# A gated graph layer on one core: the new gate and the convolution's end products summed in PSUM

## The chip, the core and the metric

The kernel runs on one core of a Trainium2 chip. The metric is the device time of one execution in microseconds (us). A core has a matrix engine (TensorE, in the profile PE, with its weight loads as PEld), a vector engine (VectorE, DVE), a scalar engine for activation functions (ScalarE, ACT), GpSimd (POOL) and a queue engine (SyncE, SP). Matrix products land in PSUM[...]; everything else lies in SBUF or in device memory. An engine runs its instructions in their order, and waits on semaphores for the others.

## The reference

There are B = 32 graphs of N = 512 nodes with D = 256 features, all fp32. Each x is normalised and clipped (h = max(layernorm(x), 0)), and a layer of three parts is added to x:

- a convolution along the nodes: a product with a 256 x 256 matrix, batch norm, relu, a convolution with 17 taps over 256 channels, batch norm, plus h, relu: x_conv;
- a message product: A = exp(-distance of three projected features) times the given mask, x_nmp = A times relu(h w_msg + b);
- a gated unit whose input is x_in = (x_conv, x_nmp) and whose state is h:

```python
r = sigmoid(gi_r + gh_r)
z = sigmoid(gi_z + gh_z)
nn_ = tanh(gi_n + r * gh_n)
return (1.0 - z) * nn_ + z * x
```

Here gi are products of x_in (512 inputs) and gh products of h (256 inputs). Only the n gate needs its two parts apart, since r multiplies the second.

## The kernel before

Features lie on partitions and nodes along the free axis. One fp32 matmul of 512 columns shows as two rows in the profile.

**An order written by a planner.** While the program is built, five generators ("rows", "begins", "graphs", "conv", "gates") are advanced one piece at a time, and what a piece emits stands in that order on each engine. The planner keeps its own account of time: `now` for TensorE, `dve.free` and `act.free` for VectorE and ScalarE. A generator yields a time from which it can go on, or a condition. Of those able to go on the planner takes the one that is furthest behind its pace. `later(t, f)` puts a small piece off until the account reaches t, and `fill` adds VectorE's background work (operands, sums) while its queue reaches less than 1.5 us ahead. On the chip nothing but this order and the semaphores is left.

**Convolution (`convolution`, L737; `summed`, L595).** The 17 taps are computed by a fast scheme: the rows are cut into seven groups, and each group has 25 products of transformed weights and inputs. In the first group a product is one bank. In the other six a product has three parts. First `psb` (tile ps_b, a bank of its own in pool `bps`) takes the middle term, and ScalarE copies it to `mid` in SBUF (L803). Then the two end products go to the two banks of `ps_c` (L806 to L808). The finished pair is handed to `summed`, where `both` (L619) adds `mid` to both halves with one VectorE instruction into `n` or `z`. Further VectorE additions, listed in SUMS and run as background, build the outputs y.

**Messages (`graph`, L969).** Per graph: eight message matmuls, then factors of the distance, `kernel_exp` (L861) with four matmuls into four banks (ps_b and three banks of pool `gps`) and four exponentials, masking on VectorE, and the gather products.

**Gates (`gates`, L1003).** Per graph and half o of the features: the products of r, of the hidden part of n (ps_h), of z, and of the input part of n (ps_n). Each takes a bank ps_acc of pool `acc`, which has two. ScalarE takes tanh of r and z, and halves and biases ps_h in place. VectorE computes r = (r + 1) ps_h into SBUF (`reset_hidden`, L1101), then adds ps_n to it (`mix`, L1117), ScalarE takes tanh of r (`mix_next`, L1035), and VectorE makes the output (`mix_last`, L1042). In the very last half the n products are cut into 384 and 128 columns, and VectorE prepares a part of the output early (`mix_ahead`, L1065).

PSUM's eight banks are: one in bps, two in acc, three in gps, two in cps (two bufs for the first group, later one buf of two banks).

Of the kernel before, what the change touches and what calls it, by code (L numbers as in the profile page):

```python
# [8 lines left out]
F32 = mybir.dt.float32  # L9
# [4 lines left out]
P = 128  # L14
# [34 lines left out]
def kernel(  # L49
# [46 lines left out]
    dram = ctx.enter_context(tc.tile_pool(name="dram", bufs=1, space=bass.MemoryType.DRAM))  # L96
    bps = ctx.enter_context(tc.tile_pool(name="bps", bufs=1, space=PSUM))
    acc = ctx.enter_context(tc.tile_pool(name="acc", bufs=2, space=PSUM))
    gps = ctx.enter_context(tc.tile_pool(name="gps", bufs=3, space=PSUM))
# [485 lines left out]
    SUMS = []  # L585
    summed_to = 0
    read = 0

    def sum_all(to=1e9):
        nonlocal summed_to  # L590
        while SUMS and summed_to < to:
            summed_to += 1
            SUMS.pop(0)()

    def summed(g):  # L595
# [10 lines left out]
        def add(dst, a, b, op=ALU.add):  # L606
            SUMS.append(lambda: dve.tensor_tensor(dst, a, b, op=op))

        def copy(dst, src, scale):
            SUMS.append(lambda: later(  # L610
                dve.free + 0.1, lambda: act.activation(dst, src, AF.Copy, scale=scale)
            ))

        def more(dst, a, k, b, op=ALU.add):
            SUMS.append(
                lambda: dve.scalar_tensor_tensor(dst, a, k, b, op0=ALU.mult, op1=op)
            )

        def both(dst, got):  # L619

            ps, mid = got
            if mid is None:
                act.activation(dst, ps, AF.Copy)
                return
            dve.tensor_tensor(
                dst.rearrange("p (h n) -> p h n", h=2), ps, mid[:, None, :].to_broadcast([P, 2, nh]),
                op=ALU.add,
            )

        for j1 in ORDER:  # L630
# [32 lines left out]
            else:  # L663
                for f in range(3):
                    add(y[:, :, f], y[:, :, f], z, ALU.subtract if (f, j1) == (1, 2) else ALU.add)
        SUMS.append(lambda: EVAC.extend(
            (dve.free + 0.3, y, g, b, o) for b in batches(g) for o in range(ND)
        ))
        yield
# [33 lines left out]
    X2, X_AT, XD = [], [], {}  # L703
    at_product = 0
    freed, made, made_at, bank_at = -1, 0, 0.0, 0.0

# [30 lines left out]
    def convolution():  # L737

        nonlocal at_product, cps

        def product(ps, *terms):


            for o in range(ND):
                matmul_sum(
                    ps[:, o * nu : (o + 1) * nu],
                    [
                        (w[:, k, i, o * P : (o + 1) * P], t[:, at + i * (nu + 1) : at + i * (nu + 1) + nu])
                        for k, t, at in terms
                        for i in range(ND)  # L750
                    ],
                )

        done, handed = None, 0.0

        def hand():
            nonlocal done, handed
            if done is not None:
                got, done = done, None
                sums.send(got)  # L760
                handed = dve.free + LAG

        for g in range(NG):
# [3 lines left out]
            if g == 1:  # L767
                first_ctx.close()
                cps = ctx.enter_context(tc.tile_pool(name="cps2", bufs=1, space=PSUM))
            for n in range(25):  # L770
                at_product = m = 25 * g + n
# [11 lines left out]
                for k in (m, m + 1):  # L783
                    if 25 <= k < len(X2) and k not in XD:
                        XD[k] = ends(X2[k], sizes(k // 25)[3])
                        X_AT[k] = dve.free + LAG
                yield max(X_AT[m], W_AT[m], bank_at if g > 0 else 0.0)
                if 25 <= m < 50:
                    third_weight(m)
                    yield W_AT[m]  # L790
                w, x2 = WS[m], X2[m]
                if g == 0:
                    ps, mid = cps.tile([P, N], F32, name="ps_c")[:, :nz], None
                    d0, d1, d2 = (x2[:, 0, :], 0), (x2[:, 1, :], 0), (x2[:, 0, :], 1)
                    product(ps[:, :nh], (0, *d0), (1, *d1))
                    hand()
                    yield now
                    product(ps[:, nh:], (0, *d1), (1, *d2))
                else:
                    psb = bps.tile([P, N], F32, name="ps_b")[:, :nh]  # L800
                    product(psb, (2, x2[:, 1, :], 0))
                    mid = cv.tile([P, NH], F32, name="mid", bufs=2)[:, :nh]
                    act.activation(mid, psb, AF.Copy)  # L803
                    hand()
                    yield handed
                    ps = cps.tile([P, 2, N], F32, name="ps_c")[:, :, :nh]  # L806
                    for k in range(2):
                        product(ps[:, k, :], (k, XD[m][:, k, :], 0))  # L808
                    del XD[m]
                WS[m] = X2[m] = None  # L810
                done = ps, mid
                if g > 0:
                    later(now + 0.3, hand)
                at_product = m + 1
                yield now
            hand()

# [43 lines left out]
    def kernel_exp(at):  # L861

        nonlocal now, bank_at
        pss = [bps.tile([P, N], F32, name="ps_b"), bank(), bank(), bank()]
        for c in range(NT):
# [103 lines left out]
    def graph(b):  # L969

        nonlocal told
        yield lambda: begun > b
# [16 lines left out]
        settle_stores()  # L989
        at = front.tile([P, NT, N], F32, name="at", bufs=1)  # L990
        kernel_exp(at)
        yield act.free + 0.3
# [10 lines left out]
    def gates(b):  # L1003
# [11 lines left out]

        def products(ps, o, g, ks, then=None, of=None):

# [3 lines left out]
            for k in ks:  # L1021
                w, at = sources[k]
                for i in range(ND):
                    matmul(
                        ps, w[:, at + i, cols(o, g)], hT[:, i, :] if k == 0 else x_in[2 * k - 2 + i],
                        start=(k == of[0] and i == 0), stop=(k == of[-1] and i == ND - 1),
                    )
                if k == ks[-1] and then is not None:
                    then()
                if k == 2 and o == ND - 1 and g == 2:  # L1030
                    load_sums(b + 1, 0)
                    load_sums(b + 1, 1)
                yield now

        def mix_next(r, z, o, s):  # L1035
            act.activation(
                r[:, s], r[:, s], AF.Tanh,
                bias=vec[:, _COL["b_ih"] + 2 * ND + o : _COL["b_ih"] + 2 * ND + o + 1],
# [46 lines left out]
        for o in range(ND):  # L1085
# [9 lines left out]

            def hidden_half(ps_h):
                act.activation(ps_h, ps_h, AF.Identity, bias=bn[:, o : o + 1], scale=0.5)

            halves = []

            def reset_hidden():  # L1101
                if halves:
                    dve.scalar_tensor_tensor(r, r, 1.0, halves.pop(), op0=ALU.add, op1=ALU.mult)

            def reset_later(ps_h):
                halves.append(ps_h)
                later(act.free + 0.3, reset_hidden)
# [8 lines left out]

            def mix(s=slice(0, N)):  # L1117
                reset_hidden()
                dve.tensor_tensor(r[:, s], ps_n[:, s], r[:, s], op=ALU.add)
                later(dve.free + 0.3, lambda r=r, z=z, o=o: mix_next(r, z, o, s))  # L1120

# [17 lines left out]

            def hidden():  # L1140
                ps = acc.tile([P, N], F32, name="ps_acc")
                yield from products(ps, o, 2, (0,), lambda: hidden_half(ps))
                reset_later(ps)

            if ps_h is not None:
                reset_later(ps_h)
            elif not is_last(o):
                yield from hidden()
            ps_z = acc.tile([P, N], F32, name="ps_acc")
            yield from products(ps_z, o, 1, (0, 1, 2), update)  # L1150
            if is_last(o):
                later(act.free + 0.2, lambda: mix_ahead(z, o))
                yield from hidden()
            if o == 0:
                load_gates(b + 1)
                load_conv(b + 1)
            else:
                residual(b + 1)
            ps_n = acc.tile([P, N], F32, name="ps_acc")
            if b < B - 1 or o < ND - 1:  # L1160
                yield from products(ps_n, o, 2, (1, 2) if o == 0 else (2, 1), mix)
                continue

            for s in (slice(0, N - P), slice(N - P, N)):
                if s.start > 0:
                    ps_n = acc.tile([P, N], F32, name="ps_acc")
                for j in range(2 * ND):
                    matmul(
                        ps_n[:, s], wih[:, j, cols(o, 2)], x_in[j][:, s],
                        start=(j == 0), stop=(j == 2 * ND - 1),  # L1170
                    )
                mix(s)
                yield now
# [5 lines left out]
    def sum_some():  # L1179
        if not SUMS:  # L1180
            return False
# [203 lines left out]
```

## Time and profile before

| | |
|---|---|
| median of 3 runs | 2104.84 us (2104.28 to 2105.43) |
| span of the profiled execution | 2103.8 us |
| mean granted TensorE clock | 0.994 |
| last TensorE row starts | 7.2 us before the end of the span |
| DVE r<-ps_acc,r (add of ps_n), 128x512 | 63 of 690 ns |
| DVE z or n <-ps_c,mid, 128x540 | 100 of 715 ns, and 50 of 128x544 |
| ACT mid<-ps_b, 128x270 | 100 of 396 ns, and 50 of 128x272 |
| TensorE rows into ps_acc, ps_c, ps_b, ps_g of at,msg | 2304, 3200, 1264, 512 |

The page gives for every engine its busy time and the number of its instructions, then the chain of work that ended last, then groups of instructions. A group reads: line, engine, operation, output<-inputs by the program's names, shapes, count, busy us, mean ns, and the idle time ahead of it with what ended it. Most instructions here have the line of a helper (L136 matmul, L141 transpose, L127 the two engines' wrapper), so groups are told apart by their tiles. The view of waits reads: waiting group, releasing group, total us, times, longest. The timeline reads: start, length, engine, line, operation, tiles, count, and in brackets the idle time ahead.

### The profile page before, as it was taken

How to read it: one execution, taken by the hardware profiler on the slowest of the kernel's cores; microseconds unless marked ns; L12 is line 12 of the kernel's file. 1: busy time of each engine (PE TensorE's matmuls, PEld its weight loads, DVE VectorE, ACT ScalarE, POOL GpSimd, SP SyncE). 2: the span in 40 equal slices, each digit the busy share in tenths (PEclk: the TensorE clock that was granted, in tenths of full speed). 3: DMA queues.
4: the chain of work that ended last, by engine and by line, in shares of the span. 5: the costliest groups of instructions: out<-in, count | busy, mean ns of one | idle time of the engine just before them, and what ended most of it. 6: DMA issues, size and time to landing. Idle time of an engine off the chain costs nothing.

```text
span 2103.8 us, 25938 instructions
## 1 busy us (share of the span) xinstructions
PE 2056.0 (98%) x8776; PEld 1260.3 (60%) x8776; DVE 1509.8 (72%) x2662; ACT 730.9 (35%) x1280; POOL 335.2 (16%) x582
## 2 busy tenths in 40 slices
PE   9999899999999999999999999999999999999998
PEld 5887466665666546656566665456665666654443
DVE  6887499886799668878488865588985877763333
ACT  6543532226322254222443222533224432133111
POOL 2000112112111021011111101211111110112111
PEclk9999999999999999999999999999999999999999
DMA  7446687777875767677776777777777655624332
GB/s 279 162 145 203 249 256 202 199 210 209 228 212 162 223 172 201 175 195 195 227 184 172 189 201 181 217 172 210 211 181 193 180 162 157 170 72 109 86 91 40
DMA packets 546436, 383.07 MB, mean 182 GB/s; under 512 B 456576, under 2 KB 473472, under 8 KB 545664
## 3 DMA queue, kind: packets, MB, share of 16 engines
q1 hardware_dynamic: 512992, 282.17, 51.3%
q0 software_dynamic: 28624, 86.01, 13.0%
q10 hardware_dynamic: 4688, 13.24, 1.6%
q8 instruction: 70, 1.15, 0.2%
q14 instruction: 62, 0.51, 0.1%
HBM read 281.95 MB, written 99.35 MB: 181 GB/s over the span
## 4 chain that ended last, share of the span: by engine, by line
PE 92%; DVE 4%; ACT 2%; DMA 1%; issue 1%; SPq 0%; POOL 0%; ACTq 0%; DVEq 0%
PE ps_acc L136 47%; PE ps_g L136 20%; PE ps_c L136 15%; PE ps_b L136 6%; PE ps_g L141 1%; PE ps_b L867 1%; ACT r L127 1%; DVE gg L127 1%; DVE at L127 1%; DVE y L127 0%; DVE z L127 0%; PE ps_acc L146 0%; ACT y L127 0%; DVE x L127 0%; ACT at L127 0%
## 5 line engine op out<-in xcount | busy, mean ns | idle before, releaser
L136 PE MATMUL ps_acc<-hTb,whh 128*128 128x512 f32 x768 | 357.6, 596 | 13.8 <-ACT r L127 13.5
L136 PE MATMUL ps_acc<-xconv,wih 128*128 128x512 f32 (+1 forms) x772 | 361.8, 591 | 0.0
L136 PE MATMUL ps_acc<-xnb,wih 128*128 128x512 f32 (+1 forms) x772 | 358.6, 591 | 0.0
L136 PEld LDWEIGHTS ps_c<-xd,w 128*128 128x128 f32 x2400 | 294.3, 191 | 31.6 <-issue 27.4
L136 PE MATMUL ps_c<-xd,w 128*128 128x135 f32 (+1 forms) x2400 | 303.5, 279 | 1.9 <-DVE n L127 1.6
L1078 POOL DMA_DIRECT2D out_dram<-res x252 | 164.0, 657 | 634.0 <-DVE res L127 559.4
L136 PEld LDWEIGHTS ps_acc<-hTb,whh 128*128 128x128 f32 x768 | 139.7, 190 | 173.7 <-issue 135.6
L136 PEld LDWEIGHTS ps_acc<-xconv,wih 128*128 128x128 f32 x772 | 142.8, 190 | 158.2 <-issue 156.3
L136 PEld LDWEIGHTS ps_acc<-xnb,wih 128*128 128x128 f32 x772 | 142.7, 190 | 157.1 <-issue 154.7
L136 PE MATMUL ps_g<-at,msg 128*128 128x512 f32 x512 | 228.8, 596 | 1.5 <-DVE at L127 1.5
L136 PEld LDWEIGHTS ps_b<-x,w 128*128 128x128 f32 x1200 | 157.1, 190 | 47.8 <-issue 39.7
L127 DVE TENSOR_TENSOR r<-ps_acc,r 128x512 f32<-128x512 f32 (+1 forms) x65 | 44.3, 682 | 192.5 <-PE ps_acc L136 192.5
L136 PE MATMUL ps_b<-x,w 128*128 128x135 f32 (+1 forms) x1200 | 163.6, 279 | 4.3 <-DMA w<-wd 2.2
L136 PEld LDWEIGHTS ps_g<-at,msg 128*128 128x128 f32 x512 | 96.1, 191 | 113.4 <-issue 108.6
L127 ACT ACTIVATE mid<-ps_b 128x270 f32<-128x270 f32 (+1 forms) x150 | 59.5, 396 | 290.8 <-PE ps_b L136 281.3
L127 DVE TENSOR_TENSOR msg<-ps_g,bmsg 128x256 f32<-128x256 f32 x128 | 53.9, 422 | 123.5 <-PE ps_g L136 123.3
L127 DVE SCALAR_TENSOR_TENSOR x<-x,x 128x544 f32<-128x544 f32 (+5 forms) x161 | 137.8, 856 | 2.9
L136 PE MATMUL ps_g<-hT,w 128*128 128x512 f32 (+4 forms) x288 | 119.9, 564 | 10.8 <-DMA hT<-hd 6.8
L127 DVE TENSOR_TENSOR x<-x 128x272 f32<-128x272 f32 (+5 forms) x280 | 127.4, 498 | 0.2
L136 PE MATMUL ps_g<-wmsg,hTg 128*128 128x259 f32 x496 | 123.5, 382 | 0.3 <-DVE aug L127 0.3
L127 DVE TENSOR_TENSOR xd<-x 128x544 f32<-128x544 f32 (+1 forms) x150 | 106.9, 719 | 23.1 <-PE ps_c L136 22.6
L127 ACT ACTIVATE z<-ps_acc,brz 128x512 f32<-128x512 f32 x64 | 44.0, 687 | 219.1 <-PE ps_acc L136 211.9
(124 smaller groups left out, 2563.4 us busy)
## 6 DMA issues: line engine op xcount, KB each, us to landing
w<-wd SPq DMA_DIRECT2D x125, 768.0 KB, 5.2
m_sb<-in_adj_dram SPq DMA_DIRECT2D x384, 64.0 KB, 3.3
hd<-hT POOLq DMA_DIRECT2D x32, 512.0 KB, 6.1
hT<-hd SPq DMA_DIRECT2D x32, 512.0 KB, 4.8
hTb<-hd SPq DMA_DIRECT2D x32, 512.0 KB, 5.4
xnb<-nd SPq DMA_DIRECT2D x64, 256.0 KB, 3.5
xconv<-cd SPq DMA_DIRECT2D x32, 512.0 KB, 5.6
res<-in_x_dram SPq DMA_DIRECT2D x256, 64.0 KB, 3.3
```

What stands on the lines that cost most here:

```text
L127: getattr(self.engine, name)(*tiles, **more)
L136: nc.tensor.matmul(ps, lhsT, rhs, **more)
L141: nc.tensor.transpose(ps, a, ident)
L867: nc.tensor.matmul(pss[c], gr.left[k, :], gr.right[k, :], start=True, stop=True, tile_position=(32 * c, 0),)
L1078: queue.dma_start(OB[b][:, s.start // 32 : s.stop // 32, o * P + 32 * g : o * P + 32 * g + 32], y[at, s].rearrange("i (k j) -> i k j", j=32),)
```

## The change

Values that VectorE or ScalarE wrote into a bank stay there, and further matmuls add onto them (start=False).

- Gates: VectorE writes (r + 1) ps_h back into ps_h's bank, and the input products of n are added onto it; ScalarE takes tanh straight from the bank. ps_n and VectorE's addition are gone. Ahead of the n products the generator yields until VectorE's planned time. `acc` has three banks.
- Convolution: the middle term goes into the first bank of ps_c, ScalarE copies it into the second, and the end products are added onto both. ps_b and `mid` are gone; `both` is now one ScalarE copy of the pair, and the next product waits for it. One seed matmul at the start of the second group writes the second bank once.
- `kernel_exp` takes its fourth bank from `acc` in the first group and from `ps_c` later, with two flags that keep it and a product apart.
- Sums in SUMS carry the time from which they may run.
- The very last half computes ps_h in two parts (384 and 128 columns), with n's products added after both.

```diff
-    bps = ctx.enter_context(tc.tile_pool(name="bps", bufs=1, space=PSUM))
-    acc = ctx.enter_context(tc.tile_pool(name="acc", bufs=2, space=PSUM))
+    acc = ctx.enter_context(tc.tile_pool(name="acc", bufs=3, space=PSUM))
...
-        def both(dst, got):
-
-            ps, mid = got
-            if mid is None:
-                act.activation(dst, ps, AF.Copy)
-                return
-            dve.tensor_tensor(
-                dst.rearrange("p (h n) -> p h n", h=2), ps, mid[:, None, :].to_broadcast([P, 2, nh]),
-                op=ALU.add,
-            )
+        def both(dst, ps):
+
+            nonlocal bank_at, sums_at
+            act.activation(dst.rearrange("p (h n) -> p h n", h=2), ps, AF.Copy)
+            bank_at = sums_at = act.free + LAG
...
+                ps = cps.tile([P, 2, N], F32, name="ps_c")
+                matmul(ps[:, 1, :NH], ident, h1[:, :NH], start=True, stop=True)
+                wide = True
...
-                    psb = bps.tile([P, N], F32, name="ps_b")[:, :nh]
-                    product(psb, (2, x2[:, 1, :], 0))
-                    mid = cv.tile([P, NH], F32, name="mid", bufs=2)[:, :nh]
-                    act.activation(mid, psb, AF.Copy)
-                    hand()
-                    yield handed
+                    in_product = True
                     ps = cps.tile([P, 2, N], F32, name="ps_c")[:, :, :nh]
+                    product(ps[:, 0, :], (2, x2[:, 1, :], 0), clear=(True, False))
+                    act.activation(ps[:, 1, :], ps[:, 0, :], AF.Copy)
+                    yield act.free + LAG
                     for k in range(2):
-                        product(ps[:, k, :], (k, XD[m][:, k, :], 0))
+                        product(ps[:, k, :], (k, XD[m][:, k, :], 0), clear=(False, False))
...
                 yield now
+                if g > 0:
+                    yield lambda: done is None
...
-        pss = [bps.tile([P, N], F32, name="ps_b"), bank(), bank(), bank()]
+        exp_waits = False
+        if not wide:
+            extra = acc.tile([P, N], F32, name="ps_acc")
+        else:
+            extra = cps.tile([P, 2, N], F32, name="ps_c")[:, 0, :]
+        pss = [extra, bank(), bank(), bank()]
...
+        if in_product:
+            exp_waits = True
+            yield lambda: not in_product
+            yield bank_at
         kernel_exp(at)
...
             def reset_hidden():
-                if halves:
-                    dve.scalar_tensor_tensor(r, r, 1.0, halves.pop(), op0=ALU.add, op1=ALU.mult)
+                while halves:
+                    ps, s = halves.pop(0)
+                    dve.scalar_tensor_tensor(
+                        ps[:, s], r[:, s], 1.0, ps[:, s], op0=ALU.add, op1=ALU.mult
+                    )
...
-            def mix(s=slice(0, N)):
-                reset_hidden()
-                dve.tensor_tensor(r[:, s], ps_n[:, s], r[:, s], op=ALU.add)
-                later(dve.free + 0.3, lambda r=r, z=z, o=o: mix_next(r, z, o, s))
+            def mix(ps_n, s=slice(0, N)):
+                later(now + 0.3, lambda r=r, z=z, o=o: mix_next(r, ps_n, z, o, s))
...
-            ps_n = acc.tile([P, N], F32, name="ps_acc")
-            if b < B - 1 or o < ND - 1:
-                yield from products(ps_n, o, 2, (1, 2) if o == 0 else (2, 1), mix)
+            if not is_last(o):
+                reset_hidden()
+                yield dve.free + 0.1
+                yield from products(
+                    ps_h, o, 2, (1, 2) if o == 0 else (2, 1), lambda: mix(ps_h), clear=False
+                )
                 continue
 
+            later(act.free + 0.2, lambda: mix_ahead(z, o))
+            parts = []
             for s in (slice(0, N - P), slice(N - P, N)):
-                if s.start > 0:
-                    ps_n = acc.tile([P, N], F32, name="ps_acc")
+                ps = acc.tile([P, N], F32, name="ps_acc")
+                parts.append((ps, s))
+                for i in range(ND):
+                    matmul(
+                        ps[:, s], whh[:, i, cols(o, 2)], hT[:, i, s],
+                        start=(i == 0), stop=(i == ND - 1), skip_group_check=True,
+                    )
+                hidden_half(ps, s)
+                reset_later(ps, s)
+                yield now
+            settle()
+            yield dve.free + 0.1
+            for ps, s in parts:
                 for j in range(2 * ND):
                     matmul(
-                        ps_n[:, s], wih[:, j, cols(o, 2)], x_in[j][:, s],
-                        start=(j == 0), stop=(j == 2 * ND - 1),
+                        ps[:, s], wih[:, j, cols(o, 2)], x_in[j][:, s],
+                        start=False, stop=(j == 2 * ND - 1), skip_group_check=True,
                     )
-                mix(s)
+                mix(ps, s)
                 yield now
...
     def sum_some():
-        if not SUMS:
+        if not SUMS or SUMS[0][0] > max(now, dve.free) + 0.1:
             return False
```

## The prediction

> **What bounds the kernel now.** I read the page's busy table first, then who TensorE waited for, then the timeline around the waits.
>
> ```profile
> span 2103.8 us, 25938 instructions
> PE 2056.0 (98%) x8776; PEld 1260.3 (60%) x8776; DVE 1509.8 (72%) x2662; ACT 730.9 (35%) x1280; POOL 335.2 (16%) x582
> PE 92%; DVE 4%; ACT 2%; DMA 1%; issue 1%; SPq 0%; POOL 0%; ACTq 0%; DVEq 0%
> ```
>
> TensorE sets the end: 98% busy and 92% of the chain. VectorE (72%) and ScalarE (35%) matter only where TensorE waits for them. The change leaves TensorE's work as it is, so it can win or lose only TensorE's stalls. How much is there? The busy figure hides short stalls, because a matmul's modelled end lies past its slot. The starts tell more:
>
> ```profile
> 2067.88 1.88 PE L136 MATMUL ps_acc<-xconv,wih 128*128 128x512 f32 x4
> 2069.60 1.88 PE L136 MATMUL ps_acc<-xnb,wih 128*128 128x512 f32 x4
> 2072.26 1.98 PE L136 MATMUL ps_acc<-hTb,whh 128*128 128x512 f32 x4 [0.78 <-ACT r L127]
> 2074.08 1.88 PE L136 MATMUL ps_acc<-xconv,wih 128*128 128x512 f32 x4
> ```
>
> Four 512-column rows take 1.72 us from start to start (0.43 each, while one row shows 0.59). After 2069.60 the next should start at 2071.32; it starts at 2072.26 and its own four take 1.82. So a shown idle of 0.78 costs 1.04: idle, plus 0.16 of modelled end, plus 0.10 of slower restart. I add 0.27 to each idle from here on. In the same way a 135-column row takes 0.115. All rows at their pace: 3040 of 512 columns x 0.43 = 1304; 3600 conv rows x 0.115 = 414; 800 x 0.111 = 89; 512 message rows x 0.217 = 111; 32 exponent groups x 1.07 = 34; 496 transposes x 0.109 = 54; 64 short conv1 rows 14: about 2020. Of the span some 84 us is stall, head (first row 1.8 us in) and tail (last row 7.2 us before the end).
>
> ```profile
> PE ps_acc L136 <- ACT r L127: 13.5, 18, 0.8
> PE ps_g L136 <- DMA hT<-hd: 6.8, 1, 6.8
> PE ps_g L136 <- ACT at L127: 4.0, 3, 1.7
> PE ps_c L136 <- DVE n L127: 1.6, 1, 1.6
> PE ps_b L136 <- ACT at L127: 1.3, 2, 0.7
> PE ps_b L867 <- ACT mid L127: 1.0, 2, 0.5
> PE ps_b L136 <- ACT mid L127: 0.8, 1, 0.8
> ```
>
> (waiting group, releaser, total us, times, longest.) The largest is one pattern: with two gate banks, the update gate takes the reset gate's bank and waits for its tanh. Two others matter as prices: TensorE re-using a bank right after an exponent group (ACT at) and right after ps_b (ACT mid).
>
> ```profile
> 231.00:239.00 8.00, 5.09 (x7) 2.28 (x8) 0.69 (x1) 1.30 (x4) 0.38 (x1) 0.57 0.98 348
> 560.00:571.00 11.00, 8.83 (x35) 5.28 (x34) 8.89 (x15) 0.99 (x2) 0.59 (x1) 0.84 0.98 302
> ```
>
> (stretch, its length, busy PE, PEld, DVE, ACT, POOL, granted clock.) After some stalls TensorE runs slower: lost 8 x 0.43 = 3.4 and 11 x 0.16 = 1.8 here; with 265 to 270 (0.66) and 740 to 748 (0.79), 8.6 us in all.
>
> [...] here an Identity into PSUM takes 663 ns and a Tanh into SBUF 687, two functions and so no clean comparison; I take the ScalarE row to PSUM at its SBUF price.
>
> **The change, part by part.**
>
> *Gates.* Every ps_r, ps_h, ps_z now has its own bank in rotation of three, and a bank is met again after at least three gate products (5.15 us). The 18 waits go: 13.5 + 18 x 0.27 = 18.4; five more that only the weight load shows about 0.6; the one DVE r wait 0.7. **-19.7.** New is that the last products of n wait for VectorE's (r+1)h written into ps_h. In the trace of before, that operation ends 3.6 us or more ahead of n's first row in nine of ten cases, since the update gate's twelve rows (5.15 us) lie between; the cover stays, VectorE has 64 adds x 0.69 = 44 us less, so 0. Queued behind a late one would be all of TensorE. The exception is the very last half: before, it ends 2.03 us after n's first row. There VectorE does four operations for the last mix (2092.21 to 2094.71) first. Now the two parts follow at 0.56 + 0.29, so n starts near 2095.3 instead of 2092.96; its rows take 3.45, part 0 is at 2097.9; tanh, multiply, transpose and add of both parts end near 2101.4 instead of 2099.6. **+1.8.**
>
> *Convolution.* VectorE loses 150 sums of 0.716 (107 us); ScalarE gets 150 copies of 540. A copy of 464 takes 561 ns and one of 270 takes 396, so 540 takes 0.63: ScalarE 731 to about 826 us. Both stay below TensorE: 0. But before, ps_b had its own bank; now product (b), ScalarE's copy, end products (xd), evacuation, next product run on one pair of banks, and so do the exponent groups. In the built order of the changed kernel I counted what stands between. Of 150 b-to-xd hand-overs 97 have exactly two gate products (1.72 us) as cover; counted from the end of b's last slot, the copy to mid was done after 0.66 us at the median and 0.70 in nine of ten cases of before; hidden. Nine have none, three have 0.55. Of xd to b seven have none, of exponents to b nine (two before), of xd to exponents two have 0.55. Prices: b's answer from ps_b L867, 0.5 + 0.27 = 0.77; exponents' 0.65 + 0.15 = 0.8 (their modelled end lies less far past the slot); xd's the former plus 0.23 of longer copy = 1.0. Sum 9 x 0.77 + 3 x 0.2 + 7 x 1.0 + 9 x 0.8 + 2 x 0.45 = 22.6. Against it fall the four like rows of before, 4.7 + 4 x 0.27 + 2 x 0.15 = 6.1. **+16.5.** Bounds: 10, if ScalarE answers as fast as its best and half the empty places have other cover in time; 40, below.
>
> *Knock-on.* Several empty places lie together (two in a row at four places), about seven half-clock windows x 1.7 = 12 against 8.6: **+3** (bounds -5 to +8). The seed matmul (two rows of 272 columns, 0.23 each) and its wait for the last copy: **+1**. Fourteen fewer warming transposes x 0.109: **-1.5**. Exponent groups directly ahead of a gps bank: four before (4.0 + 0.6), one after (1.4): **-3.2**. The 6.8 us wait for hT at 226 us came from a store that POOL issued late; the order there is reshuffled and I can't tell: halved, **-3** (bounds -7 to +7). ScalarE's copies into n and z may now wait for VectorE's additions and hold ScalarE's whole queue, gate activations and b copies too: in five of 22 cases before, the z sum followed the last y addition at once. **+3** (bounds 0 to 10). Stores and loads keep their number; SP's and POOL's queues only shift.
>
> Sum: -19.7 + 1.8 + 16.5 + 3 + 1 - 1.5 - 3.2 - 3 + 3 = -2.1. On the profiled execution 2103.8 becomes 2101.7; the runs lie 1.0 above the span (2104.84), so **2102.7 us**.
>
> **Rivals.** (1) *Near cancellation*, as summed: chance 0.42, own range 2097 to 2109. (2) *Hand-overs hidden*: half of the 22.6 and no extra half-clock windows, hT's wait gone: -2.1 - 8 - 3 + 3 - 4 + 3 = about -11, 2093. For: ScalarE is 35% busy and only 1 in 20 mid copies started later than 0.9 us after its rows. Against: nine empty places can't hide. Chance 0.25. (3) *Slower: ScalarE answers late at the hand-over inside the product*, because it is blocked by VectorE's additions or by its 1.33 us evacuations and 1.54 us y copies. Place: the 97 hand-overs with 1.72 us; it decides from an answer later than 1.7 us in one of about eight of them: 12 x 1.0 us, and as much half clock as goes with it, +12 to +20: 2116. For: the longest start of a mid copy was 4.1 us late. Against: the order was made with ScalarE's queue in view. Chance 0.25. (4) *No relief*: the bank wait returns as a wait for (r+1)h, -19.7 missing: 2122. The 3.6 us of slack speak against it. Chance 0.08.
>
> **How the numbers follow.** Within 0.2% (2100.6 to 2109.1, about what a measurement of this kernel tells from no change): 0.29 from (1), 0.03 from (2), 0.04 from (3): 0.36. Faster: 0.11 + 0.22 = 0.33. Slower: 0.02 + 0.21 + 0.08 = 0.31. The range of eight in ten takes in (2) and most of (3): 2091 to 2117.
>
> **What would show it.** Right: no "ps_acc L136 <- ACT r" left; new TensorE waits of ps_c for ACT ps_c, ACT z, ACT n and ACT at, some 25 to 30 of below 1 us; DVE about 1360, ACT about 826 us; the last TensorE row some 2 us later against the last z activation. Wrong: ps_acc rows waiting for DVE ps_acc; ps_c waits of several us with ACT waiting for DVE y or z; a long wait at the first change of convolution groups; more than ten half-clock stretches.

## The result: 0.9% slower

The changed kernel takes 2125.32 us (median of 4 runs, 2122.68 to 2126.22) against 2105.14 us. The ratio estimated from the runs is 1.0093, with a 95% interval of 1.0079 to 1.0107. Every ratio below is taken against runs of the kernel before made beside it, whose median lies between 2102.7 and 2105.1 us, so the times divided by one another don't give it exactly. The forecast was 2102.7 us with a range up to 2117, so the time lies outside it, on the slow side. The profiled execution went from a span of 2103.8 to 2123.3 us, 19.5 us more.

The page of the changed kernel, its span, busy times and the chain by engine:

```profile
span 2123.3 us, 25913 instructions
...
PE 2062.8 (97%) x8768; PEld 1265.0 (60%) x8768; DVE 1375.5 (65%) x2448; ACT 815.2 (38%) x1431; POOL 337.7 (16%) x582
...
PE 93%; ACT 2%; DMA 2%; DVE 1%; issue 1%; SPq 0%; POOL 0%; ACTq 0%; DVEq 0%
```

VectorE is 134 us less busy and ScalarE 84 us more. TensorE still sets the end. In the chain VectorE's share fell from 4 to 1%, while that of DMA rose from 1 to 2%. What TensorE waited for (waiting group, releaser, total us, times, longest):

```profile
PE ps_g L135 <- DMA hT<-hd: 14.7, 4, 7.9
PE ps_c L135 <- ACT z L126: 6.6, 4, 4.8
PE ps_c L135 <- ACT at L126: 6.0, 9, 0.7
PE ps_c L135 <- ACT n L126: 5.1, 6, 1.3
PE ps_c L135 <- ACT ps_c L126: 4.8, 9, 0.5
PE ps_c L877 <- ACT z L126: 3.1, 3, 1.3
PE ps_c L877 <- ACT n L126: 2.5, 2, 1.3
PE ps_acc L135 <- DVE ps_acc L126: 2.1, 1, 2.1
```

The gates' 13.5 us for ACT r are gone. In their place stand six kinds of wait of ps_c for ScalarE, 28.1 us in 33 shown stalls, and the wait for hT doubled from 6.8 to 14.7: one of 7.9 us near 222 us, where before had its 6.8, and a new one of 5.9 us near 767 us make up most of it.

To size this beyond the shown idle, I took each TensorE row's distance to the next row's start, less the row's own pace, and sorted the excess by what released the next row. The half-clock column is half the length of the stretches whose granted clock is 0.5 in the records, without the first and the last of the execution. It counts idle time inside the stretches too. The columns overlap a little and don't add up to the span. All values are us, with the number of stalls in brackets:

| kernel | span | gate banks for ACT r | convolution's banks for ScalarE | the same for others | hT and other DMA | other waits | half clock |
|---|---|---|---|---|---|---|---|
| before | 2103.8 | 16.7 (22) | 5.6 (8) | 4.9 | 7.0 | 7.6 | 8.5 |
| after | 2123.3 | 0.5 (1) | 34.3 (41) | 0.3 | 15.3 | 6.7 | 18.8 |

At their pace the rows take 2024.9 us before and 2023.8 after. So the gates gave back 16 us; the convolution's banks took 24 (34.6 against 10.5), DMA 8, and the slow clock 10 (7 without the idle time inside its stretches: 14.5 against 7.4).

**Two places.** The convolution's waits don't all stand where there was nothing to do. First TensorE and then ScalarE near 332 us, from the timeline of the changed kernel (start, length, engine, line, operation, tiles, count, idle ahead):

```profile
329.37 2.00 PE L135 MATMUL ps_c<-xd,w 128*128 128x135 f32 x16
331.21 1.88 PE L135 MATMUL ps_acc<-xnb,wih 128*128 128x512 f32 x4
334.38 0.69 PE L877 MATMUL ps_c<-right,left 5*128 5x512 f32 x1 [1.29 <-ACT z L126]
```

```profile
333.13 0.69 ACT L126 ACTIVATE z<-ps_acc,brz 128x512 f32<-128x512 f32 x1 [5.04 <-PE ps_acc L135]
333.72 0.61 ACT L126 ACTIVATE z<-ps_c 128x540 f32<-128x540 f32 x1
```

The last end product (xd) ends at 331.4. ScalarE has nothing to do at that time: it stands idle for 5.04 us, until 333.13. But next in its order is the tanh of z, and that needs the four gate rows that TensorE runs from 331.21 to 333.1. Only behind it comes the copy of the pair, at 333.72. The four gate rows, which should have hidden the copy, hold it back. The exponent group that needs the banks starts at 334.38.

The longest such wait, all engines of the timeline, lines left out:

```profile
467.66 2.00 PE L135 MATMUL ps_c<-xd,w 128*128 128x135 f32 x16
...
470.34 0.69 DVE L126 TENSOR_TENSOR w<-w 128x512 f32<-128x512 f32 x1 [2.85 <-DMA w<-wd]
471.59 1.22 DVE L126 TENSOR_TENSOR xconv<-xconv,hTb 128x1024 f32<-128x1024 f32 x1
472.84 1.06 ACT L126 ACTIVATE xconv<-xconv 128x1024 f32<-128x1024 f32 x1 [4.29 <-DVE xconv L126]
473.80 0.60 ACT L126 ACTIVATE z<-ps_c 128x540 f32<-128x540 f32 x1
...
474.46 1.94 PE L135 MATMUL ps_c<-x,w 128*128 128x135 f32 x7 [4.80 <-ACT z L126]
```

Here the pair is ready at 469.7. The copy stands behind a relu of xconv, that behind VectorE's addition, and that behind a sum for w that waits 2.85 us for its transfer. The next product starts at 474.46, after 4.80 us of idle.

**The clock.** In the view of stretches (stretch, length, busy PE, PEld, DVE, ACT, POOL, granted clock, DMA share, GB/s):

```profile
227.00:238.00 11.00, 8.26 (x13) 3.55 (x14) 0.69 (x1) 2.54 (x6) 0.54 (x1) 0.63 1.02 286
337.00:341.00 4.00, 4.00 (x12) 2.02 (x11) 2.06 (x4) 1.85 (x4) 0.24 (x1) 0.57 0.78 248
771.00:779.00 8.00, 6.17 (x9) 2.75 (x10) 1.48 (x1) 1.28 (x4) 2.61 (x4) 0.58 0.54 194
1354.00:1359.00 5.00, 5.00 (x8) 2.03 (x8) 4.60 (x7) 2.60 (x6) 0.78 (x1) 0.66 0.55 103
```

Seven such stretches count 18.8 us by half their length (four and 8.5 before). Those at 227 and 771 begin during waits of 7.9 and 5.9 us for hT. The one at 337 follows the stall of 1.29 us shown above and one of 0.67 us after the exponents: TensorE is busy throughout, at 0.57 of its clock. But stalls are not the whole cause: in the 3.41 us ahead of the stretch near 1355 TensorE idled for only 0.30 us, and an exponent group after a stall of 1.29 us near 833 was followed by no slow stretch. The last section comes back to this.

### The profile page after: what moved, and what is told of

Same layout as the page of the kernel before. It is cut to its first block, busy times and chain, and to the rows that moved or that the text cites. A ratio compares the mean times of both kernels' runs of the same rounds, so it can differ in the third digit from the quotient of the medians.

```text
span 2123.3 us, 25913 instructions
## 1 busy us (share of the span) xinstructions
PE 2062.8 (97%) x8768; PEld 1265.0 (60%) x8768; DVE 1375.5 (65%) x2448; ACT 815.2 (38%) x1431; POOL 337.7 (16%) x582
## 3 DMA queue, kind: packets, MB, share of 16 engines
q0 software_dynamic: 28624, 86.01, 12.9%
## 4 chain that ended last, share of the span: by engine, by line
PE 93%; ACT 2%; DMA 2%; DVE 1%; issue 1%; SPq 0%; POOL 0%; ACTq 0%; DVEq 0%
PE ps_acc L135 46%; PE ps_c L135 24%; PE ps_g L135 20%; DMA hT<-hd 2%; PE ps_g L140 2%; PE ps_c L877 1%; ACT at L126 0%; PE ps_acc L145 0%; DMA w<-wd 0%; ACT z L126 0%; PE ps_acc L877 0%; DMA vec<-in_vecs_dram 0%; ACT n L126 0%; ACT part L126 0%; PE ps_g L877 0%
## 5 line engine op out<-in xcount | busy, mean ns | idle before, releaser
L135 PE MATMUL ps_acc<-hTb,whh 128*128 128x512 f32 (+1 forms) x772 | 357.3, 592 | 0.0
L135 PEld LDWEIGHTS ps_c<-xd,w 128*128 128x128 f32 x2400 | 300.2, 191 | 70.4 <-issue 56.3
L135 PEld LDWEIGHTS ps_c<-x,w 128*128 128x128 f32 x2000 | 253.5, 192 | 88.7 <-issue 54.7
L135 PE MATMUL ps_c<-x,w 128*128 128x135 f32 (+2 forms) x2000 | 262.4, 280 | 17.5 <-ACT z L126 6.3
L126 DVE TENSOR_TENSOR o_sb<-hTb,r 128x512 f32<-128x512 f32 x63 | 43.5, 690 | 211.3 <-ACT r L126 211.3
L126 ACT ACTIVATE ps_c<-ps_c 128x270 f32<-128x270 f32 (+1 forms) x150 | 57.6, 384 | 206.1 <-PE ps_c L135 206.1
L135 PE MATMUL ps_g<-hT,w 128*128 128x512 f32 (+4 forms) x288 | 121.3, 570 | 14.7 <-DMA hT<-hd 14.7
L126 ACT ACTIVATE h<-ps_g,bn_shift,bn_scale 128x252 f32<-128x252 f32 (+4 forms) x208 | 85.8, 487 | 84.8 <-PE ps_g L135 84.7
```

What stands on the lines that cost most here:

```text
L126: getattr(self.engine, name)(*tiles, **more)
L135: nc.tensor.matmul(ps, lhsT, rhs, **more)
```

## The experiments

Three theories. **A**: the changed hand-overs cost what they must, since the convolution now has one pair of banks. **B**: ScalarE's copy of the pair is emitted too late, behind gate work, and that is where the time goes. **C**: what I call the gates' new yield, the wait until VectorE's planned time ahead of n's products, keeps the gates from supplying rows between the hand-overs. A fourth possibility stands beside them: that another order of the same work simply happens to be this much slower. The expectations, each written before its run, use letters of their own and say beside each letter what it stands for.

### The parts alone

*e1_gates_alone*: the gates' part on the kernel before; `acc` stays at two banks, the convolution with ps_b as it was.

```diff
             def mix(s=slice(0, N)):
-                reset_hidden()
-                dve.tensor_tensor(r[:, s], ps_n[:, s], r[:, s], op=ALU.add)
...
+                reset_hidden()
+                yield dve.free + 0.1
+                yield from products(
+                    ps_h, o, 2, (1, 2) if o == 0 else (2, 1), lambda: mix(ps_h), clear=False
+                )
```

> The gates' part alone: n summed in ps_h's bank, the convolution as before, two gate banks. Theory A (the shared convolution banks are what costs): without the third bank the wait of the update gate for the reset gate's tanh stays (about 20 us of stall), the conv has no waits for ACT z or n, and the time is within 8 us of before, 2097 to 2113. Theory B (the gates' sums in PSUM cost): TensorE waits for DVE ps_acc or for the n tanh in ps_acc, and the time is over 2115.

2130.43 us, ratio 1.0126 (1.011 to 1.0141). Its waits:

```profile
PE ps_acc L136 <- ACT r L127: 17.2, 22, 0.8
PE ps_c L136 <- DVE z L127: 5.4, 2, 4.4
```

With two banks the waits for ACT r stay, more of them than before, and the part alone already costs 26 us. Neither theory of the expectation fits: the time lies above A's range, yet no row waits for (r + 1) ps_h but in the very last half (2.1 us), so the arithmetic isn't late. What is new are waits of other banks for VectorE (its sums, and w and aug), as if the order had less to choose from.

*e2_conv_alone*: the convolution, the exponents and the third bank as in the changed kernel, the gates' arithmetic as before. Against the changed kernel:

```diff
-            def mix(ps_n, s=slice(0, N)):
+            def mix(s=slice(0, N)):
+                reset_hidden()
+                dve.tensor_tensor(r[:, s], ps_n[:, s], r[:, s], op=ALU.add)
```

> The convolution's part and the third gate bank, gates' arithmetic as before (ps_n and VectorE's addition). Theory A: the ps_c waits stay as in the changed kernel (ACT z and n some 15 us, ACT at and ACT ps_c some 6 us each), the ACT r wait is gone, 2115 to 2130. Theory B: the convolution's part costs little, near or below 2105.

2122.66 us, 1.0089 (1.007 to 1.0108). The ACT r waits are gone (0.5 us left by the table's measure), and still it is 18 us above the kernel before. The convolution's banks wait 17.2 us for ScalarE in 19 stalls, where some 27 were expected; DMA takes 19.7, half clock 18.8.

```profile
PE ps_g L135 <- DMA hT<-hd: 18.3, 5, 7.6
PE ps_c L135 <- ACT at L126: 6.7, 10, 0.7
PE ps_acc L135 <- ACT xconv L126: 5.9, 4, 3.6
```

*e3_two_banks*: the changed kernel with two gate banks.

```diff
-    acc = ctx.enter_context(tc.tile_pool(name="acc", bufs=3, space=PSUM))
+    acc = ctx.enter_context(tc.tile_pool(name="acc", bufs=2, space=PSUM))
```

> The changed kernel with two gate banks in place of three. Theory A: the ACT r wait of some 14 us idle (20 us with restarts) comes back on top of the changed kernel, about 2140 (2132 to 2150). Theory B (the third bank never was worth much, the waits only moved): within 6 us of 2125.

2141.2 us, 1.0178 (1.0163 to 1.0193), 16 us above the changed kernel. PE, VectorE and ScalarE run the changed kernel's order, instruction by instruction, so no other order can be the cause: this is the third bank's gain by itself. The wait comes back, and the other columns hardly move (33.8 us for the convolution's banks, 14.8 for DMA, the same half clock):

```profile
PE ps_acc L135 <- ACT r L126: 9.4, 12, 0.8
```

By the table's measure the wait is about 11 of the 16 us; where the rest goes was not traced. So the third bank does its work. Without its 16 us the change costs 36, and both the convolution's part and the gates' part lose when alone.

### Is it only another order?

A change of the planner's account by a hair gives another order of the same instructions (apart from at most 36 rows of `keep_warm`'s transposes). `LAG` is the planner's allowance for an answer, 0.6 us; `now` starts at 5.0.

```diff
-    LAG = 0.6
+    LAG = 0.65
```

*e5_before_lag* is this on the kernel before, *e5c_before_lag55* has 0.55, and *e5b_before_start* has `now = 5.25`; *e6_after_lag* and *e6b_after_start* are the same on the changed kernel.

> The kernel before with one number of the planner's account changed (LAG 0.60 to 0.65 us); the same instructions in another order. Theory D (the order of before is an unusually good one, and any replanning brings one-off waits with half-clock stretches behind them): 2110 to 2130. Theory A (only what the change adds costs): within 5 us of 2105.

> The kernel before with the planner's clock started at 5.25 in place of 5.00 us; the same instructions in another order. Theory D: 2110 to 2130. Theory A: within 5 us of 2105.

> The kernel before replanned once more, with LAG 0.55: the fourth plan of the same instructions. Theory D in its narrower form (a plan alone is worth some 8 us either way): 2097 to 2117, with the ACT r wait at about 17 us and the conv-bank waits for ScalarE at 4 to 6 us in every plan.

> The changed kernel with LAG 0.65 in place of 0.60. Theory D: the one-off waits (hT from memory, the 4.8 us for ACT z) move or go and others come, anywhere in 2108 to 2132, the short ps_c waits for ACT stay about 20 us. Theory A: within 5 us of 2125.

> The changed kernel with the planner's clock started at 5.25. Theory D: anywhere in 2108 to 2132. Theory A: within 5 us of 2125.

| order | kernel before | changed kernel |
|---|---|---|
| as it is | 2105.14 | 2125.32 |
| LAG 0.65 | 2117.34 (1.0069, 1.0054 to 1.0084) | 2139.9 (1.0179, 1.0164 to 1.0194) |
| now 5.25 | 2100.07 (0.999, 0.9981 to 0.9999) | 2123.8 (1.0107, 1.009 to 1.0125) |
| LAG 0.55 | 2101.23 (0.9985, 0.9978 to 0.9992) | |
| mean | 2105.9 | 2129.7 |

Orders differ by up to 17 us, as much as a part of this change is worth, so one order alone says little about a mechanism. LAG 0.65 on the changed kernel lies above the widest range expected of it (2132). But pair by pair the changed kernel is 20 to 24 us slower, and its spread from slowest to fastest doesn't reach the other's. So the loss is not one unlucky order. The changed kernel's three orders all have 34 to 38 us on the convolution's banks; the four of the kernel before have 4 to 6 there for ScalarE. The orders are not equally far apart, though: by the rows in the traces (`keep_warm`'s transposes left out), `now` 5.25 changes TensorE's order in the changed kernel only between 36 and 200 us, LAG 0.65 up to 1260 us; in the kernel before the three reach to 856, 1593 and 1709 us. The changed kernel's three are thus two orders and a variant of one.

### B: the copy emitted too late

`hand` is what emits the pair's copy. The changed kernel puts it off by 0.3 us in the planner's account, and by then other pieces may have been emitted on ScalarE.

```diff
                 if g > 0:
-                    later(now + 0.3, hand)
+                    hand()
```

> The changed kernel with the pair's copy put into ScalarE's order directly after the end products, ahead of a gate's tanh that waits for later rows. Theory A (the copies stand behind a tanh that waits for the very rows meant as cover): the waits of 1.3 us for ACT z and n go, the one of 4.8 us too if it stood behind the xconv relu, 8 to 15 us less, 2110 to 2117. Theory C (the pair of banks is shared by too much whatever ScalarE's order is): within 5 us of 2125.

*e4_hand_first*: 2116.35 us, 1.0054 (1.0039 to 1.0069), 9 us better than the changed kernel. (The traced execution is the fastest of its four, which go from 2112.8 to 2118.8 us.) The copy in the timeline now starts 0.26 us after the slot of the last end product (331.37):

```profile
331.63 0.62 ACT L126 ACTIVATE z<-ps_c 128x540 f32<-128x540 f32 x1 [1.30 <-PE ps_c L135]
```

I measured this for all 150 pairs from the second group on, from the end of the last xd row's slot to the copy's start. In the changed kernel the copy is over 1 us late in 52, in one of ten by 3.3 us or more, at most 5.1. With the copy at once it is late in 5. (Before, VectorE's sum was over 1 us late in 103, by 1.6 at the median; only one row of TensorE waited for it, for 1.6 us, because the next product had ps_b.) The copy of b inside the product is in time in both: 6 and 5 of 150 are over 1 us late, the median is 0.26.

B is confirmed as a mechanism: the late copies go. Its size is less sure. The 9 us are a little under half of the loss, but they come from one order, and orders alone differ by up to 17. And 27.6 us on the convolution's banks remain, in 40 stalls:

```profile
PE ps_c L135 <- ACT ps_c L126: 6.4, 12, 0.5
PE ps_c L877 <- ACT z L126: 4.8, 6, 1.2
PE ps_c L135 <- ACT z L126: 4.4, 7, 0.8
```

These are short ones: the answer comes at once, but no row stands in the meantime, in e4's order at 12 hand-overs from b to xd, 9 from xd to b and 6 from xd to exponents.

### C: the gates' yield

Ahead of n's products the gates yield `dve.free + 0.1`. That is the end of all that VectorE has been given, background sums included, and the planner keeps VectorE supplied at least 1.5 us ahead. So the gates can count as unable to go on when (r + 1) ps_h has long been ready. *e10_reset_at* yields the planned end of that operation instead:

```diff
             def reset_hidden():
+                nonlocal reset_at
...
+                    reset_at = dve.free + 0.1
...
                 reset_hidden()
-                yield dve.free + 0.1
+                yield reset_at
```

> The changed kernel, but the gates wait for the planned end of the one operation that writes (r+1)h into the bank, not for the planned end of all that VectorE has queued by then. Theory E (that yield makes the gates unable to go on just when the convolution needs cover, and so empties the hand-overs): conv-bank waits for ScalarE fall from 34 us to about 17, as in the run of the convolution alone, and the ACT r wait stays away, 2100 to 2112, order noise of some 8 us aside. Theory A (the shared banks cost it whatever the gates yield): within 8 us of 2125.

2124.46 us, 1.0087 (1.0069 to 1.0104): no gain, where 2100 to 2112 was expected. Yet the named wait falls as expected, from 34.3 to 12.9 us on the convolution's banks; in the order, 2 of the products' hand-overs from b to xd and none from xd to b stand empty, against 9 and 7. The time went elsewhere:

```profile
PE ps_g L135 <- DMA hT<-hd: 23.3, 6, 8.2
PE ps_acc L135 <- ACT xconv L126: 9.4, 3, 4.4
PE ps_c L135 <- ACT at L126: 7.3, 11, 0.7
```

DMA rises from 15.3 to 24.9 us, other waits from 6.7 to 18.2, half clock from 18.8 to 23.9 (14.5 to 16.0 without idle time). In the trace the longest wait for hT has its load issued behind x and mask loads on SP's queue; first SP, then TensorE:

```profile
1343.04 6.05 SPq L917 DMA_DIRECT2D x_sb<-xd  x8
...
1351.88 2.51 SPq L338 DMA_DIRECT2D m_sb<-in_adj_dram  x4
1354.49 2.28 SPq L210 DMA_DIRECT2D hT<-hd  x1
```

```profile
1360.20 5.24 PE L135 MATMUL ps_g<-hT,w 128*128 128x512 f32 x6 [8.20 <-DMA hT<-hd]
```

*e14_reset_at_lag* and *e15_reset_at_start* are this kernel in two more orders (LAG 0.65 and `now` 5.25).

> The changed kernel with the gates' own wait, replanned with LAG 0.65. Theory E: conv-bank waits for ScalarE stay at 10 to 20 us (against 34 to 38 in three plans of the changed kernel), the waits for hT and xconv (35 us in the first plan) fall, 2100 to 2118. Theory A: conv-bank waits above 25 us or the time at 2124 again.

> The same, replanned with the planner's clock started at 5.25. Theory E: conv-bank waits 10 to 20 us, 2100 to 2118. Theory A: above 25 us or 2124 again.

2128.66 (1.0128, 1.011 to 1.0146) and 2129.22 us (1.0124, 1.0105 to 1.0142), with 20.0 and 12.8 us on the banks, 22.2 and 19.0 for DMA, and other waits of 13.6 and 18.4. Both times miss the 2100 to 2118 expected. The waits on the banks are again fewer than in the changed kernel's orders, and those for DMA more. Against the changed kernel in the same plan the edit is worth 11.2 us with LAG 0.65 and costs 5.4 with `now` 5.25 (the order of e10 but for the first 200 us). So C alone brings nothing that stands clear of the order.

*e13_gates_reset* is the same edit on e1, the gates alone with two banks.

> The gates' part alone with the same yield mended (convolution as before, two gate banks). Theory E: the waits that this part had beyond the one for ACT r (DVE z, DVE aug, DVE w, some 17 us at the convolution's banks) go, 2100 to 2112. Theory D (they are one-off effects of a new order): still within 8 us of 2130, or anywhere between.

2103.79 us, 0.9994 (0.9986 to 1.0002), against 2130.43 for e1. All that the gates' part alone cost is gone, and nothing is gained:

```profile
PE ps_acc L136 <- ACT r L127: 15.3, 21, 0.8
PE ps_g L136 <- DMA hT<-hd: 7.1, 2, 5.5
```

So the new arithmetic of the gate costs nothing here and, with two banks, brings nothing; the 26 us went with the yield. I have this in one order only.

### B and C together

*e11_reset_hand* is e10 with `hand()` at once. *e12_all_fixes* adds two small edits: the exponent group always waits in the plan for the pair's copy, and VectorE's early part for the last half (`mix_ahead`) goes behind (r + 1) ps_h. *e18_all_but_reset* is e12 without the edit of the yield.

```diff
-        if in_product:
+        if wide:
             exp_waits = True
...
-            later(act.free + 0.2, lambda: mix_ahead(z, o))
             parts = []
...
             settle()
             yield dve.free + 0.1
+            later(act.free + 0.2, lambda: mix_ahead(z, o))
```

> As the run with the gates' own wait, and the pair's copy put into ScalarE's order directly after the end products. Theory E: conv-bank waits fall below 15 us, no waits of 1.3 us for ACT z or n behind a tanh left between end products and the next product; some remain ahead of exponent groups; 2092 to 2106. Theory A: above 2112.

> As the last, and the exponent group always waits in the plan for the pair's copy, and in the very last half VectorE writes (r+1)h before the last mix's four operations. Theory E: conv-bank waits below 10 us, the last half's 2.1 us wait for DVE ps_acc below 1 us: 2088 to 2102, faster than the kernel before. Theory A: above 2112.

> All mends but that of the gates' wait. Theory E (the gates' yield on all of VectorE's queue is what empties the hand-overs): conv-bank waits 20 to 32 us and 2105 to 2120. Theory F (ScalarE's order is what counts, the yield is not): below 15 us, 2088 to 2098.

| kernel | us | ratio to before | banks for ScalarE | DMA | other waits | half clock |
|---|---|---|---|---|---|---|
| after | 2125.32 | 1.0093 (1.0079 to 1.0107) | 34.3 (41) | 15.3 | 6.7 | 18.8 |
| e4, B | 2116.35 | 1.0054 (1.0039 to 1.0069) | 27.6 (40) | 8.5 | 16.0 | 8.5 |
| e18, B and the small edits | 2113.87 | 1.005 (1.0034 to 1.0067) | 25.7 (35) | 10.7 | 13.1 | 11.9 |
| e10, C | 2124.46 | 1.0087 (1.0069 to 1.0104) | 12.9 (20) | 24.9 | 18.2 | 23.9 |
| e11, B and C | 2095.64 | 0.9943 (0.992 to 0.9965) | 13.6 (16) | 11.3 | 8.4 | 11.9 |
| e12, all | 2090.27 | 0.9925 (0.9906 to 0.9944) | 12.3 (11) | 10.5 | 7.0 | 8.5 |

B brings 9 us (11 with the small edits), C alone 1, both 30 to 35. A falls: the same change, with the same instructions on TensorE and one pair of banks, is faster than the kernel before once both are mended. The waits on the banks are 12.3 us in e12, not below 10 as expected. VectorE and ScalarE are as busy in e12 as in the changed kernel; what fell are TensorE's stalls, though one of 4.2 us for ACT n and the waits for hT remain. From its page (span 2088.2 us) and its waits:

```profile
PE 2049.9 (98%) x8768; PEld 1259.9 (60%) x8768; DVE 1375.2 (66%) x2448; ACT 817.1 (39%) x1431; POOL 338.0 (16%) x582
```

```profile
PE ps_g L135 <- DMA hT<-hd: 9.8, 4, 7.1
PE ps_c L135 <- ACT n L126: 5.5, 2, 4.2
...
PE ps_acc L135 <- DVE ps_acc L126: 0.9, 1, 0.9
```

*e16_all_lag* and *e17_all_start* are e12 in two more orders.

> The version with all four mends, replanned with LAG 0.65. If its gain over before is of the mends, 2085 to 2102; if it was a lucky order, 2105 to 2120.

> The version with all four mends, replanned with the planner's clock started at 5.25. If its gain is of the mends, 2085 to 2102, with conv-bank waits for ScalarE near 13 us; if the two plans so far were lucky, 2105 to 2120.

2099.69 us (0.998, 0.9972 to 0.9988) and 2094.06 (0.9953, 0.9936 to 0.9969). The three orders average 2094.7, against 2105.9 for the four of the kernel before and 2129.7 for the three of the changed one. So the mended change is worth about 11 us, 0.5%, by these orders; the 0.75% of e12 itself is partly a good order. The estimate is loose: `now` 5.25 changes e12's order of TensorE only between 36 and 201 us and LAG 0.65 only between 117 and 595, so all three are one order from there on. Another order of the later part is e11's, which differs from e12's between 988 and 1803 us and is also faster than the kernel before.

**What stays open.** Why C without B brings nothing. In e10 the pair's copy is late in 61 of 150, and the convolution is held in the plan until it is emitted; that the work put in its place runs ahead of its loads would explain the waits for hT and xconv, and e11, where they fall to 11.3 and 8.4, fits it. But no run separates the plan from the loads' own queue, so this is argued and not shown.

## Why the prediction was wrong

**What held.** The gates: 19.7 us of waits were to go; the table has 16.2 less and e3 measures 16 for the bank, some 3.5 less than summed. No row waits for (r + 1) ps_h but in the very last half. That half's start was put 2.3 us later; the timeline of the changed kernel shows 2.10 of idle there:

```profile
2109.02 1.90 PE L135 MATMUL ps_acc<-hTb,whh 128*128 128x384 f32 x8
...
2113.02 1.56 PE L135 MATMUL ps_acc<-xconv,wih 128*128 128x384 f32 x4 [2.10 <-DVE ps_acc L126]
```

VectorE at 1375 us (said: 1360), ScalarE at 815 (826), the copy of 540 at 618 ns (630). And the prices of empty hand-overs: nine of b to xd cost 6.4 us (6.9 said), nine of exponents to b 6.5 (7.2). The copy of b inside the product was in time in all but 6 of 150, as said.

**What failed first: cover.** The convolution's step took rows between xd and the next user of the banks as cover for the copy, priced the empty places, and put 1.5 us on five with 0.55 us of cover. But ScalarE's order often had ahead of the copy the very work that reads those rows: of the seven such stalls for a pair's copy four stand behind the tanh of z on the rows meant as cover, two behind the copies of just-made transposes, one behind evacuations and the relu of xconv. So hand-overs with rows between cost 10.3 us, and the seven empty ones of xd to b 10.5 instead of 7.0, one of them 4.8 us. In sum 34.3 us where 22.6 were written. What was subtracted was too small as well: the table has 10.5 us of before at these banks, 4.9 of it waits for others than ScalarE, where 6.1 were taken. The two errors partly cancel. Net +24 against +16.5. The 3 us for ScalarE being held had the right engine and the wrong holder: gate activations and other copies whose inputs were not there yet, not VectorE's y and z additions. That this needs no late engine, only a place in a queue, was missed: the argument looked at ScalarE's 35% of busy time and at how soon b's copy had answered.

**Second: the knock-on terms.** hT was put at -3 and came out at +8; half clock at +3 (seven windows) and came out at +10 (eleven windows of 3.4 us; +7 without the idle time inside them). Both lie beyond their bounds (+7 and +8), and together they miss by 19 us, more than the convolution's 5. They may partly hang on the cover: with the copy at once (e4) DMA is at 8.5 us and half clock at 8.5 again, in one order, while other waits rise from 6.7 to 16.0. So in the sum these two are most of the miss, and why they grew stays partly open.

**Third: a term that wasn't there.** The gates' new yield was priced by whether the operation is late on the chip, at 0. It was never asked what the yield does to the planner, which sees the gates as unable to go on. Wherever the pair's copy was not in the way this was worth 20 to 27 us (e1 to e13 26.6, e4 to e11 20.7, e18 to e12 23.6). The empty hand-overs that it leaves were counted in the built order and priced, so it is little of the miss in the sum (e10: 1 us). What was missed is that they could be avoided.

| step | said | measured in the changed kernel |
|---|---|---|
| gates | -19.7 | -16.2 |
| convolution, with ScalarE held | +19.5 | +24.1 |
| hT and DMA | -3 | +8.3 |
| half clock | +3 | +10.3 |

**The rivals.** Near cancellation, held the likeliest, fell. Of the slower ones, the forecast of 2116 named ScalarE's answer inside the product (b to xd), blocked by VectorE. The engine was right, the place wrong: b's copies were late in 6 of 150 cases, the pair's in 52, at the end of the product. No relief (2122 us) had almost the right time by another cause: the gates' wait did go and did not come back. Hand-overs hidden (2093) is what e12 shows to be reachable, not what was built; its sum was also wrong by its own terms (half of 22.6 is 11.3, not 8, and its two additions of 3 name no reason). Of the signs named as speaking against the forecast, two came true in part: one ps_c wait of several us (4.8), with ScalarE waiting for VectorE's xconv and not for y or z; and eleven half-clock windows, in seven stretches.

## What to carry to other kernels

When a buffer's release moves to another engine, look up what stands ahead of the releasing instruction in that engine's order: an idle engine is late if the next in its queue waits, and work that is meant as cover can be the very thing it waits for (here ScalarE stood idle for 5.04 us, and the copy behind the tanh of z started 2.3 us late). In an order written by a planner, ask of each new yield what the planner can no longer choose meanwhile; the wait on the chip may be zero and the cost tens of us (here no row waited for (r + 1) ps_h outside the very last half, and the yield cost 20 to 27 us wherever the copy was not in the way). Try a mend in several orders and together with the others: here two mends brought 9 and 1 us alone and 30 together, while a meaningless shift of a constant moved the time by up to 17. And look how far such a shift really changes the order: here some rejoined the old one after 200 us.

## What the runs showed of the hardware

- By the records of the granted clock (1.0 or 0.5) of the kernel before and the changed one, every slow stretch but the last, which the end cuts off, is 3.41 us long or a multiple of it, and within a trace the starts lie whole steps of 3.413 us apart (224.82 and 337.46 us in the changed kernel: 33 steps). Some start after little idle time. The step ahead of the one at 337.46 had 1.0 us of idle, that ahead of 1354.63 only 0.30; yet one with 1.59 us of idle (552.5 us, before) was followed by full clock. Ahead of four of the seven stretches of the changed kernel (337, 382, 576, 1355) the step holds an exponent group, whose rows have 5 input partitions of 128, ahead of the other three it is idle for 3.0 us or more. But 27 of its 32 exponent groups are followed by a step at full clock (the fifth of the others stands ahead of the first stretch, near 30 us), so what decides is not shown.
- ScalarE's Copy of 128x270 out of PSUM takes 384 ns into PSUM (ps_c<-ps_c) and took 396 ns into SBUF (mid<-ps_b). That is the clean comparison that was missing ahead of the change. The copy into PSUM is 12 ns shorter, 3%:

```profile
L126 ACT ACTIVATE ps_c<-ps_c 128x270 f32<-128x270 f32 x100 | 38.4, 384 | 140.1 <-PE ps_c L135 140.1
L126 ACT ACTIVATE z<-ps_c 128x540 f32<-128x540 f32 x60 | 37.1, 618 | 61.9 <-PE ps_c L135 59.4 <-issue 2.6
```

- VectorE's (r + 1) ps_h of 128x512 takes 691 ns into PSUM (ps_acc<-r,ps_acc) and took 681 into SBUF (r<-r,ps_acc): in place in the bank costs 10 ns more.
- All runs with the convolution's part have the seed matmul on the second bank. None leaves it out, so whether the sum in that bank needs it is not shown.
